# Window attention followed by product-key experts: the layer norms' last step moved from VectorE to ScalarE

## The chip, the cores and the metric

The kernel runs on one core of one Trainium2 chip. The metric is the device time of one execution in microseconds (us). Before the change the median of three runs is 1780.35 us (1779.88 to 1781.02).

## The reference

The input `x` has 16 sequences of 512 tokens of 128 numbers. Two layers are added onto it, each behind a layer norm over the 128 numbers of a token, without weights:

```python
def _layernorm(x, axis=-1, eps=1e-05):
    m = jnp.mean(x, axis=axis, keepdims=True)
    v = jnp.var(x, axis=axis, keepdims=True)
    return (x - m) / jnp.sqrt(v + eps)
...
x = x + _L0_attn_ref(_layernorm(x, axis=-1), L0_attn_w_qkv, L0_attn_w_proj)
x = x + _L0_ffn_ref(_layernorm(x, axis=-1), ...)
```

The first layer is attention with 16 heads of 8 numbers, where each token sees the tokens at most 128 places away. The second normalises its input again over all 8192 tokens (so the statistics of every token are needed before any of it can start), scores two sets of 32 keys for each of 8 heads, takes the eight best sums, and weighs the rows of 1024 experts with them.

## The kernel before, in words

The kernel has two stages. The first, some 830 us, is the attention with both layer norms; the second, the experts, starts when the last sequence's second norm is done. Both norms, and so all of the change, lie in the first stage.

A sequence is called a batch here, with index `b`. It has 4 token blocks (`NQ`) of 128 tokens, one token to a partition, and its heads fall into 4 groups (`NG`) of 4. A unit `n` is one group of one batch. The main loop (L498 to L541) walks through steps `s`: `n, u = divmod(s, 4)`, `b, g = divmod(n, 4)`, so 16 steps to a batch. A step traces:

- `greatest` (L363) for the unit two ahead: four score matmuls into `s_ps` (two PSUM buffers), each followed on VectorE (DVE) by one custom instruction, `masked` (L378), which adds the band mask and takes the row's maximum, `mx`;
- `exponentials` (L407): two pairs of matmuls into `e_ps` (two buffers), each pair followed on ScalarE (ACT) by one Exp into `pT` (L421); GpSimd (POOL) then cuts the sides of the band (L429);
- `weigh` (L435), two steps behind: matmuls of `pT` into `o_ps`;
- at `u == 1` `greatest_rows` (L396: transposes into `mT_ps`, a copy on ACT, a DMA), at `u == 2` `divide` (L453: transposes into `t_ps`, then `rec` and `attn` on DVE), and once a batch `project` (L468);
- one step of the generator `preparing`, which makes the batch two ahead ready: `prepare(b + 2)` (L315) normalises it, transposes it, multiplies it by the q, k and v weights and splits q and k into three bf16 pieces on POOL (`pieces`);
- one step of the generator `beside`, a chain of odd jobs: `ln_stats` of the batches of a later chunk of four (first norm, tiles with "a"), `second_norm` of the last chunk (tiles with "b", from L482), and early on `weights_of_experts`.

`ln_stats` (L271) makes a mean and a variance per token with two DVE instructions a block (L277, L278), then for the whole chunk the square root on ACT (L282) and its reciprocal on DVE (L283). `normalised_T` (L288), called by `prepare` (tiles `xn`) and by `second_norm` (tiles `xi`), does the last step of the norm for the four blocks of a batch with four DVE `tensor_scalar` (L292), yields, transposes them on TensorE (PE) into `ps_m` and copies them out on ACT (L300). The tile `xn` comes from a pool of two buffers that both norms share; `ps_m` is one PSUM buffer which all of `xn`, `xi`, `q`, `k`, `v`, `mT`, `t_ps`, `a_ps` and `y_ps` share. `second_norm` goes on with the statistics `bn_st` over tokens (L488) and a DMA.

What sets the order: matmuls and transposes are kept in program order by `mm` and `tr` (L166 to L171). The instructions of DVE, ACT and POOL in this stage are put in order beforehand by the planner of the framework, which gives an engine, by its own estimate of times, the ready instruction that is earliest in the program; on the chip each engine then runs its list strictly in that order. The waits for data and for free buffers are added to it.

Of the kernel before, what the change touches and what calls it, by code (L numbers as in the profile page):

```python
# [15 lines left out]
AF = mybir.ActivationFunctionType  # L16
ALU = mybir.AluOpType
# [26 lines left out]
def kernel(  # L44
# [13 lines left out]
    nc = tc.nc  # L58
# [3 lines left out]
    NQ = T // P  # L62
# [17 lines left out]
    xs = []  # L80
    for b in range(B):
        t = keep.tile([P, NQ, D], F32, name=f"x_{b}")
# [70 lines left out]
    with ExitStack() as at:  # L153
# [16 lines left out]
        def tr(out, in_, eye):  # L170
            tc.keep_in_program_order(nc.tensor.transpose(out, in_, eye))  # L171
# [99 lines left out]
        def ln_stats(bs, name, into):  # L271

            n = len(bs) * NQ
            mv = ln.tile([P, CH * NQ, 2], F32, tag=f"mv{name}", name=f"mv{name}_{bs[0]}", bufs=3)
            for i in range(n):
                st = ln.tile([P, 6], F32, tag="st", name=f"st{name}_{bs[0]}_{i}", bufs=4)
                nc.vector.bn_stats(st, xs[bs[i // NQ]][:, i % NQ])  # L277
                nc.vector.bn_aggr(mv[:, i], st)  # L278
                if i % NQ == NQ - 1:
                    yield  # L280
            rstd = ln.tile([P, CH * NQ], F32, tag=f"rs{name}", name=f"rs{name}_{bs[0]}", bufs=3)
            nc.scalar.activation(rstd[:, 0:n], mv[:, 0:n, 1], AF.Sqrt, bias=eps)  # L282
            nc.vector.reciprocal(rstd[:, 0:n], rstd[:, 0:n])  # L283
            for i, b in enumerate(bs):
                into[b] = mv[:, i * NQ : i * NQ + NQ], rstd[:, i * NQ : i * NQ + NQ]
            yield

        def normalised_T(b, mv, rstd, dst, tag):  # L288

            xn = w2.tile([P, NQ, D], F32, tag="xn", name=f"{tag}_{b}")  # L290
            for t in range(NQ):
                nc.vector.tensor_scalar(  # L292
                    xn[:, t], xs[b][:, t], mv[:, t, 0:1], rstd[:, t : t + 1],
                    ALU.subtract, ALU.mult,
                )
            yield
            ps = ps_m.tile([P, NQ, P], F32, tag="m", name=f"{tag}_ps_{b}")
            for t in range(NQ):
                tr(ps[:, t], xn[:, t], ident)
            nc.scalar.copy(dst, ps.rearrange("p t q -> p (t q)"))  # L300
            yield
# [13 lines left out]
        def prepare(b):  # L315

            xnT = w2.tile([P, T], F32, tag="xnT", name=f"xnT_{b}")
            yield from normalised_T(b, *norms.pop(b), xnT, "xn")
            for what, w in (("q", wqT), ("k", wkT)):
                ps = ps_m.tile([P, T], F32, tag="m", name=f"{what}_ps_{b}")  # L320
                mm(ps, lhsT=w, rhs=xnT, start=True, stop=True)
                full = w2.tile([P, T], F32, tag="full", name=f"{what}f_{b}")
                nc.scalar.mul(full, ps, 1.0 / math.sqrt(DK) if what == "q" else 1.0)
                yield
                pc = w2.tile([P, 3, T], BF16, tag="pc", name=f"{what}p_{b}")
                yield from pieces(full, pc, f"{what}_{b}")
                via = dr.tile([3, P, T], BF16, tag=f"{what}v", name=f"{what}v_{b}")
                nc.sync.dma_start(via.rearrange("s c t -> c s t"), pc)
                pieced[what, b] = via
            va = vaug[b % 3]  # L330
            if b < 3:
                nc.gpsimd.memset(va, 0.0)
                nc.gpsimd.memset(va[:, :, :, DK : DK + 1], 1.0)
            v_ps = ps_m.tile([P, NQ, NH, DK], F32, tag="m", name=f"v_ps_{b}")
            for t in range(NQ):
                mm(
                    v_ps[:, t].rearrange("p h k -> p (h k)"),
                    lhsT=xnT[:, t * P : (t + 1) * P], rhs=wvT, start=True, stop=True,
                )
            nc.scalar.copy(va[:, :, :, 0:DK], v_ps)  # L340
            yield
# [140 lines left out]
        def second_norm(bs):  # L482
            into = {}
            yield from ln_stats(bs, "b", into)
            for b in bs:
                t = w2.tile([P, T], F32, tag="xiT", name=f"xiT_{b}")
                yield from normalised_T(b, *into[b], t, "xi")
                nc.vector.bn_stats(bn_st[:, b], t)  # L488
                nc.sync.dma_start(xT[b], t)
# [5 lines left out]
        for _ in ln_stats([0], "a", norms):  # L495
            pass
        preparing, beside, ending = iter(()), iter(()), iter(())
        for s in range(-2 * NG * NQ, (NU + 1) * NQ):  # L498
            n, u = divmod(s, NQ)
            b, g = divmod(n, NG)  # L500
            if g == u == 0 and b + 2 < B:
                preparing = prepare(b + 2)
            if g == u == 0 and b == -2:
                beside = chain(ln_stats([1], "a", norms), ln_stats([2, 3], "a", norms))
# [351 lines left out]
    for i in range(NB + 1):  # L856
        b, t = divmod(i, NQ)
# [86 lines left out]
```

## Time and profile before

| | |
|---|---|
| median of 3 runs | 1780.35 us |
| the profiled execution | 1777.3 us |
| its span, first to last instruction | 1775.6 us |
| first stage: up to the end of the last norm | about 836 us |
| PE / DVE / ACT / POOL busy in 60 to 836 us | 666.6 / 589.5 / 479.9 / 398.9 us |
| `tensor_scalar` of L292 | 128 in all, 64 `xn` and 64 `xi` |
| mean duration of those in 60 to 836 us | 452 ns (`xn`), 453 ns (`xi`) |
| ACT table loads at L282 and L421 | 8 and 7, 1.283 us each |

The span is what the profile covers; some 1.7 us of the execution lie around it. From one projection's copy (L475) to the next, batches take 46.5 us when nothing of the second norm runs beside them, 57.2 and 56.7 us in the two windows that hold most of a `second_norm` together with statistics of the next chunk, 48.3 us in the two after those, and 50.6 us in the window with a `second_norm` alone.

A line of the profile that names a group reads: line of the kernel, engine, operation, output<-inputs with their shapes, number of instructions, busy time and mean duration, idle time of the engine in front of them and what ended it. In a timeline a line starts with the start and the length in us; in brackets stands the idle time in front. "xN" means N instructions of a kind in a row.

### The profile page before, as it was taken

The numbers are of one execution on the slowest core, as the hardware profiler recorded it, in microseconds if no ns is written. First come the engines' busy times: TensorE is split into PE (matmuls) and PEld (weight loads), VectorE is DVE, ScalarE is ACT, GpSimd is POOL, SyncE is SP. The second block draws the span as 40 slices with busy tenths as digits, with TensorE's granted clock in tenths as the row PEclk, the third lists the DMA queues.
The fourth block names the chain that finished last, engine by engine and source line by source line (L and its number), as shares of the span: only waits on it lengthen the run. The fifth ranks groups of instructions, "written<-read, shape, count | busy, mean of one in ns | idle before, by whom it ended". The sixth has DMA issues, their size and how long they took to land.

```text
span 1775.6 us, 49257 instructions
## 1 busy us (share of the span) xinstructions
PE 1476.7 (83%) x16752; PEld 856.5 (48%) x16752; DVE 1406.9 (79%) x8087; ACT 1146.9 (65%) x2018; POOL 1035.6 (58%) x1634
## 2 busy tenths in 40 slices
PE   4888887888788888886888888888888887888877
PEld 1444443444344444443455555555555555555555
DVE  6767778877787778775888888888888888888884
ACT  1566666656666566556776767776776767777763
POOL 7455554555555555543566666666666666666664
PEclk9999999999999999998889999999999999999999
DMA  6332222222122222210000000000000000000000
GB/s 176 89 104 70 71 68 66 86 74 70 56 86 74 70 71 78 81 55 25 8 8 14 8 8 14 14 8 8 14 14 14 8 8 14 14 8 8 8 8 14
DMA packets 87565, 75.03 MB, mean 42 GB/s; under 512 B 12177, under 2 KB 83089, under 8 KB 87185
## 3 DMA queue, kind: packets, MB, share of 16 engines
q1 hardware_dynamic: 86480, 71.61, 13.3%
q8 instruction: 133, 2.18, 0.5%
q14 instruction: 120, 0.97, 0.2%
q10 hardware_dynamic: 832, 0.26, 0.1%
HBM read 49.28 MB, written 20.97 MB: 40 GB/s over the span
## 4 chain that ended last, share of the span: by engine, by line
DVE 34%; PE 31%; POOL 16%; ACT 9%; issue 7%; SPq 2%; DMA 1%; DVEq 0%; POOLq 0%; ACTq 0%
DVE masked L378 9%; POOL g L578 6%; PE o_ps L168 6%; DVE idx L578 5%; PE s_ps L168 4%; DVE row L578 4%; PE off_ps L578 4%; PE w_ps L578 4%; PE up_ps L578 3%; POOL word L578 3%; DVE place L578 3%; DVE top L578 3%; ACT pT L421 2%; DVE mine L578 2%; DVE best L578 2%
## 5 line engine op out<-in xcount | busy, mean ns | idle before, releaser
L378 DVE CUSTOM_DVE_ANT_0 masked<-s_ps,band 128x384 bf16<-128x384 f32 (+1 forms) x1024 | 500.3, 489 | 150.0 <-PE s_ps L168 65.7
L421 ACT ACTIVATE pT<-e_ps 128x512 f32<-128x512 f32 (+1 forms) x512 | 357.9, 702 | 239.8 <-PE e_ps L168 224.9
L429 POOL TENSOR_SCALAR_AFFINE_SELECT pT<-pT 128x512 f32<-128x512 f32 x384 | 237.2, 635 | 337.4 <-ACT pT L421 337.4
L168 PE MATMUL s_ps<-kst,qst 128*128 128x384 bf16 (+1 forms) x1024 | 313.6, 307 | 87.2 <-DVE mx L378 66.0
L578 POOL TENSOR_TENSOR cols<-mine,wT 64x512 f32<-64x512 bf16 x256 | 273.0, 1066 | 20.9 <-DVE mine L578 4.0
L578 PEld LDWEIGHTS w_ps<-cols,row 128*64 128x64 f32 x8192 | 248.6, 138 | 25.4 <-POOL cols L578 14.4
L578 PE MATMUL w_ps<-cols,row 128*64 128x32 f32 x8192 | 252.7, 223 | 6.0 <-POOL cols L578 5.0
L578 POOL TENSOR_TENSOR g<-g,gel 128x512 f32<-128x512 f32 x128 | 163.6, 1278 | 151.4 <-ACT g L578 115.3
L168 PE MATMUL e_ps<-qst,kst 128*128 128x384 bf16 (+1 forms) x1024 | 225.3, 303 | 4.1 <-ACT pT L421 4.0
L168 PE MATMUL o_ps<-pT,vaug 128*32 128x384 f32 (+1 forms) x2048 | 191.6, 446 | 5.4 <-POOL pT L429 5.4
L578 ACT ACTIVATE row<-off_p,one 128x512 f32<-128x512 bf16 x256 | 184.8, 722 | 8.3
L578 ACT ACTIVATE off_p<-off_ps 128x512 bf16<-128x512 f32 x256 | 149.0, 582 | 41.6 <-PE off_ps L578 41.6
L578 DVE FIND_INDEX8 idx<-top,sim 128x8 uint32<-128x32 f32 x1024 | 167.3, 210 | 0.0
L168 PEld LDWEIGHTS <-qst 128*128 128x128 bf16 x1024 | 100.8, 99 | 133.0 <-issue 88.1
L168 PEld LDWEIGHTS <-kst 128*128 128x128 bf16 x1024 | 97.2, 98 | 122.9 <-issue 94.7
L578 DVE TENSOR_TENSOR row<-x_ps,nums_p 128x1024 f32<-128x1024 f32 x128 | 151.0, 1228 | 0.0
L578 POOL TENSOR_TENSOR cand<-top 128x512 f32<-128x512 f32 x64 | 68.2, 1066 | 140.1 <-DVE top L578 140.1
L578 PE MATMUL dn_ps<-xt,key_inT 128*64 128x256 f32 x1024 | 133.9, 398 | 17.3 <-ACT off_p L578 16.5
L578 PE MATMUL up_ps<-g,key_out_sb 64*128 64x256 f32 x1024 | 131.4, 398 | 0.0
L578 PE MATMUL off_ps<-p_bf,ident_bf 128*128 128x512 bf16 x256 | 113.9, 445 | 19.4 <-ACT p_bf L578 19.4
L578 DVE TENSOR_TENSOR word<-word,shift 128x128 uint32<-128x128 uint32 x64 | 23.5, 367 | 123.3 <-POOL word L578 123.3
L578 PEld LDWEIGHTS up_ps<-g,key_out_sb 64*128 64x128 f32 x1024 | 97.1, 193 | 44.5 <-issue 34.6
(141 smaller groups left out, 2488.8 us busy)
## 6 DMA issues: line engine op xcount, KB each, us to landing
qst<-qv SPq DMA_DIRECT2D x576, 32.0 KB
kst<-kv SPq DMA_DIRECT2D x576, 32.0 KB
qv<-qp SPq DMA_DIRECT2D x16, 384.0 KB
kv<-kp SPq DMA_DIRECT2D x16, 384.0 KB
x<-in_L_attn_x_dram SPq DMA_DIRECT2D x16, 256.0 KB
xT<-xiT SPq DMA_DIRECT2D x16, 256.0 KB
xt<-xT SPq DMA_DIRECT2D x16, 256.0 KB
out_dram<-o_sb SPq DMA_DIRECT2D x16, 256.0 KB
```

Source lines behind the costliest of these rows:

```text
L168: tc.keep_in_program_order(nc.tensor.matmul(*args, **kw))
L378: nc.vector.tensor_tensor_reduce(masked[:, 0:w], s, band.rearrange("p u k -> p (u k)")[:, from_u : from_u + w], 1.0, LOWEST, ALU.add, ALU. ...
L421: nc.scalar.activation(pT[:, 2 * pair : 2 * pair + 2, 0:w], e_ps[:, :, 0:w], AF.Exp)
L429: nc.gpsimd.affine_select(out=side, in_=side, compare_op=ALU.is_ge, fill=0.0, base=0, pattern=[[0, 4], [sign, P]], channel_multiplier=-sign,)
L578: return lambda *args, **kw: tc.keep_in_program_order(op(*args, **kw))
```

## The change

`ln_stats` gets one more small DVE instruction for a chunk, which makes -mean/std of every token in the place of the means. `normalised_T` lets ACT compute `Identity(x * rstd + shift)` with two per-partition operands in the place of DVE's subtract and multiply, and yields after each two blocks, so that it takes three steps of its generator instead of two. Nothing else changes in the text; what follows a normalisation in `preparing` and `beside` moves back by one step for each.

```diff
             nc.vector.reciprocal(rstd[:, 0:n], rstd[:, 0:n])
+            nc.vector.scalar_tensor_tensor(
+                mv[:, 0:n, 0], mv[:, 0:n, 0], -1.0, rstd[:, 0:n], ALU.mult, ALU.mult
+            )
             for i, b in enumerate(bs):
-                into[b] = mv[:, i * NQ : i * NQ + NQ], rstd[:, i * NQ : i * NQ + NQ]
+                into[b] = mv[:, i * NQ : i * NQ + NQ, 0], rstd[:, i * NQ : i * NQ + NQ]
             yield
...
-        def normalised_T(b, mv, rstd, dst, tag):
+        def normalised_T(b, shift, rstd, dst, tag):
             xn = w2.tile([P, NQ, D], F32, tag="xn", name=f"{tag}_{b}")
             for t in range(NQ):
-                nc.vector.tensor_scalar(
-                    xn[:, t], xs[b][:, t], mv[:, t, 0:1], rstd[:, t : t + 1],
-                    ALU.subtract, ALU.mult,
+                nc.scalar.activation(
+                    xn[:, t], xs[b][:, t], AF.Identity, bias=shift[:, t : t + 1],
+                    scale=rstd[:, t : t + 1],
                 )
-            yield
+                if t % 2:
+                    yield
             ps = ps_m.tile([P, NQ, P], F32, tag="m", name=f"{tag}_ps_{b}")
```

## The prediction, made before the result was known

> **What bounds the kernel now.** All 128 edited instructions lie before 836 us, so I read the page for the engines' sums, then the waits between 60 and 836 us, then DVE's timeline. No engine is full: of these 776 us PE is busy 666.6, DVE 589.5, ACT 479.9. The waits say who holds whom:
>
> ```profile
> ACT pT L421 <- PE e_ps L168: 218.1, 266, 1.9
> ...
> PE s_ps L168 <- DVE mx L378: 60.4, 197, 4.8
> DVE masked L378 <- PE s_ps L168: 56.7, 158, 2.1
> ...
> PE q_ps L168 <- DVE attn L464: 6.8, 13, 0.7
> ```
>
> (waiter, releaser; us in total, times, longest.) PE waits for DVE about as long as DVE for PE: two engines coupled by the two `s_ps` buffers. ACT mostly waits for matmuls; PE waits for ACT little. So an instruction taken off DVE is worth at best its time, and about half of it where the pair alternates; one put on ACT has room.
>
> Next, what a `tensor_scalar` really costs on DVE. The timeline, first two neighbours without one, then two with one in between:
>
> ```profile
> 292.65 0.56 DVE L378 CUSTOM_DVE_ANT_0 masked<-s_ps,band 128x384 bf16<-128x384 f32 x1
> 293.13 0.08 DVE L378 DVE_READ_ACCUMULATOR2_ANT mx<- 128x1 f32 x1
> 293.36 0.56 DVE L378 CUSTOM_DVE_ANT_0 masked<-s_ps,band 128x384 bf16<-128x384 f32 x1
> ```
> ```profile
> 305.69 0.34 DVE L292 TENSOR_SCALAR xi<-x,mvb,rsb 128x128 f32<-128x128 f32 x1
> 305.94 0.54 DVE L378 CUSTOM_DVE_ANT_0 masked<-s_ps,band 128x384 bf16<-128x384 f32 x1
> 306.42 0.08 DVE L378 DVE_READ_ACCUMULATOR2_ANT mx<- 128x1 f32 x1
> 306.42 0.34 DVE L292 TENSOR_SCALAR xi<-x,mvb,rsb 128x128 f32<-128x128 f32 x1
> 306.68 0.54 DVE L378 CUSTOM_DVE_ANT_0 masked<-s_ps,band 128x384 bf16<-128x384 f32 x1
> ```
>
> `masked` follows `masked` after 0.71 us, and after 0.74 us with a `tensor_scalar` between: DVE stands still for some 0.15 us behind every read of the accumulator (293.21 to 293.36) anyway, and the 0.34 us instruction, which overlaps its neighbours, fills that hole. With 256 columns it is 0.58 and 0.60. So a slotted one costs 0.02 to 0.03 us, not the 0.45 us of its mean. Only those cost that are stretched or come in a row.
>
> Quiet batches (46.5 us each) hold no L292 at all: the two `xn` buffers are filled ahead. What is to be gained lies around the second norms. There the chain of the window 255 to 335 us has such a row on it:
>
> ```profile
> 269.17 0.42 DVE masked L378
> 269.59 1.68 DVE xi L292 x5
> 271.27 0.09 DVE mva L278
> ...
> 274.58 0.23 DVE mva L278 x2
> 274.83 0.32 ACT rsa L282
> 275.20 0.13 issue
> 275.34 0.38 DVE masked L378
> ```
>
> For 5.8 us no `masked` runs: five `xi` and the statistics of the next chunk, then the square root on ACT.
>
> **The change part by part.**
>
> *Removed from DVE, fully on the chain:* the row of five, 1.68 us, and its twin at 468.18: 3.4 us. What comes next there is the statistics, which move up by as much.
>
> *Removed from DVE, on the pair:* 14 single ones last 0.56 to 0.75 us, mean 0.69, 0.35 over the 0.34 of the others: 4.9. Four in a row at 105.37 keep `masked` away for 1.96 us from the start of the read, where 0.23 is usual: 1.7. At 308.69 and 506.75 three in a row and one that waits for its buffer keep `masked` away until 312.06; its own matmul starts at 310.69 and takes 0.27, so 1.1 each: 2.2. Some 45 slotted ones by 0.03: 1.3. Together 10.1; as PE and DVE wait for each other equally, half of it counts: 5.0. Bounds: nothing, and all 10.1.
>
> *Added on ACT:* 128 Identities of 128x128 with two per-partition operands. No row has this. From below: Sqrt with a per-partition bias, 128x16, 0.308 us; from above: `xb`, Identity 128x512 with one such operand from SBUF, 0.706 us. A line between these two gives 0.40 at 128 columns; with a second operand that no row shows I take 0.45 (an estimate), so 57.6 us, 48.6 of it for the 108 between 60 and 826 us. ACT is idle for some 296 of 776 us there, which hides most. What is not hidden: ACT starts an instruction each 776/751 = 1.03 us, so 0.45/1.03 = 44% of the 108 delay one that becomes ready meanwhile, by half of 0.45: 10.5 us of delays. ACT stands on the chain for about a tenth (`pT` 5.5%, `mT` 2.3%), and what it delays is partly waited for by PE through `e_ps` and `ps_m`: I let a quarter count, 2.6 us, between a tenth (1.0) and all (10.5).
>
> The Trainium skill, "ScalarE: Activation LUTs", "What ACT_TABLE_LOAD costs", gives 280 ns + 0.833 ns an element with one pointer operand and 93 ns more for a second; an estimate from it is 0.48 us each, 61 us in all and 2.8 for my 2.6. Its "Rules for kernel authors" speaks against the change: additions and multiplications belong on VectorE, which is faster at them. By that rule alone the change loses 128 x (0.48 - 0.34) = 18 us, which would take the sum to 1798; it counts no engine's free time.
>
> *Table loads:* none is added. At 837.52 `xb`'s Identity runs after the Sqrt of `bn_a` at 835.34 with no load between, and `qf`'s scaled copy runs among the Exps.
>
> *Added on DVE:* 11 instructions of at most 128x16, nearest row the reciprocal, 0.18 to 0.25 us. Ten are slotted like the above or stand beside waits: 0.3 us. If that cover is gone, 2.5.
>
> *The end of the stage,* where nothing covers anything:
>
> ```profile
> 831.47 0.18 DVE L283 RECIPROCAL rsb<-rsb 128x4 f32<-128x4 f32 x1 [0.36 <-ACT rsb L282]
> 831.69 1.12 DVE L292 TENSOR_SCALAR xi<-x,mvb,rsb 128x128 f32<-128x128 f32 x4
> 832.15 0.89 PEld L171 LDWEIGHTS xi_ps<-ident,xi 128*128 128x128 f32 x4 [3.32 <-issue]
> ```
>
> Four `tensor_scalar` take 1.12; one small instruction more, a hop to ACT and four Identities at about 0.35 apart take about 0.2 + 0.15 + 1.5. That is 0.7 more, but the transposes run block by block behind them and were the slower part before (the four take 1.15), so I take 0.6 (0.2 to 1.0). At the start of the kernel the same holds for the first `xn`, but there `xnT` stands on ACT behind a square root that ends at 11.09, and POOL's pieces bound what follows: 0.
>
> *Moved:* all behind a normalisation in `prepare` goes one step later: transposes of `xn` from `u=1` to 2, q from 2 to 3, v from 0 to 1, POOL's eight pieces and the two DMAs on SP's queue with them. The last yield is then the 14th of 16 steps, and the loads by `lay` come at the fourth step of the next batch, so no load gets late. At `u=1` `xn` shared `ps_m` with `mT`; now v does. At `u=2` q waited for `attn`; now `xn` does. One collision for one: 0, with 0.5 us a batch either way as bound (the two waits' own means, 0.6 and 0.5), 7 us for 14 batches. `second_norm` of four batches takes 17 steps instead of 13, and the `ln_stats` chained behind it five: 22 of the 24 there are.
>
> *Sum:* -3.4 - 5.0 + 2.6 + 0.3 + 0.6 = -4.9 us. The profiled execution (1777.3, span 1775.6) would take 1772.4; on the median of the runs, which is 3.05 above it, 1775.4.
>
> **The rivals.**
>
> *Nothing to be seen.* Only the rows of five are worth anything (3.4) and the costs of 3.5 eat them: 1780.4. For it: slotted ones are nearly free. Against it: the batches at 48.3 us, with 11 L292 in them, are 1.8 over the quiet ones.
>
> *Slower: ACT waits for the `xn` buffer with Exps queued behind it.* A third tile in a row must wait for PE's transposes of the one before last. On DVE this wait shows as `xn <- PE xi_ps`, 0.31 to 0.64 us, five times in the stage. On ACT `pT` and the copies that free `ps_m` queue behind it, and PE, in its fixed order, comes to those transposes only after the matmuls that need `e_ps` free. At 0.64 for each of the 15 `xi` tiles in the stage it is 9.6 on top: 1785.0. It undoes the gain from 0.33 a tile and shows as slower from 0.57. For it: the planner's times were wrong there already. Against it: PE waits for ACT's `pT` only about 1 us in each of these windows now.
>
> *The step's shift.* v at `u=1` waits for `mT`, and `xn` at `u=2` waits as long as q did, while q meets the projection's copy: one collision more a batch, 0.6 by 14: 1783.8, at the edge of what shows. DVE's and ACT's lists are planned anew as well, so this can come with either sign.
>
> **How the numbers follow.** About 0.2%, 3.6 us, is what a measurement of this kernel can tell from no change. Forecast 0.40, nothing to be seen 0.22, ACT's wait 0.26, the shift 0.12, half of it on each side of the limit. So faster 0.40, same 0.28, slower 0.32. The forecast's own range is 1768 (all 13.5 of DVE, ACT's least) to 1776.8. The range over the cases goes to 1789, where ACT's delays count whole and only the rows of five are gained (1780.35 - 3.4 + 10.5 + 0.9 = 1788.4), and starts at 1767.
>
> **What would show it.** Right: in the profile after, the stretch without `masked` near 270 us is about 1.7 us shorter, the 57 us windows fall by 2 to 4 us, the 46.5 us ones stay, PE's wait for `mx` falls by some 5 us, and the Identities last about 0.45 us without table loads beside them. Wrong: quiet batches change by over 0.5 us (the shift); ACT's L292 group carries idle time ended by PE (the buffer); PE's waits for `pT`, `mT` or `qf` grow by more than 3 us; or the row of statistics in front of the square root grows.

## The result, and the profile after

| | before | after |
|---|---|---|
| median of 12 runs each, us | 1783.49 (1779.30 to 1786.06) | 1783.05 (1777.80 to 1790.62) |
| ratio after/before, 95% interval | | 1.0007 [0.9990, 1.0024] |
| profiled execution, its span, us | 1777.3, 1775.6 | 1784.43, 1782.7 |
| end of the first stage, us | 838.3 | 841.8 |
| DVE busy, ACT busy over the span, us | 1406.9, 1146.9 | 1367.0, 1193.8 |

No change that can be told. The forecast was 4.9 us faster; the work did move, some 40 us of it off DVE and 47 us onto ACT. This is the page's line of the engines after:

```profile
PE 1481.5 (83%) x16752; PEld 858.9 (48%) x16752; DVE 1367.0 (77%) x7970; ACT 1193.8 (67%) x2146; POOL 1036.1 (58%) x1634
```

**A finer measure than the whole time.** Behind the last norm the instruction lists of the two kernels are the same on every engine, so what the change does must show before it. I use the *end of the first stage*: the start of the first matmul into `sim_ps`, at 838.3 us before and 841.8 after. The copies `aT` of the projections cut the stage into a head, 15 windows and a tail. All stage ends below are of one profiled execution of each kernel. A window's length comes back to 0.1 us from one execution to the next, except for the two windows of 57 us. A repeat of the kernel before (one execution, 1780.56 us, nothing edited) shows why those differ:

> The kernel before, once more, for how well the profile's first stage repeats: if the stage is set by the lists alone, it ends within 0.5 us of 838.29 and each window from one projection's copy to the next within 0.3 us of its length.

It measured 836.9 for the stage. Its two long windows take 56.20 and 56.08 us at a mean granted clock of 0.97, where the first execution took 57.17 and 56.71 at 0.94; its other 13 windows agree within 0.02 us, the head differs by 0.8 and the tail by 0.4. So neither half of the expectation held, and the reason is the clock and the two ends. In the tables below a window stands with its clock where that is not 1.00, and a difference between 0.94 and 0.97 (here 1.0 and 0.6 us) needs no edit. What lies behind the stage scatters more: with the same lists it took 937.3 us before, 942.0 in the repeat and 940.9 after.

Windows in us, "first" and "second" being the two that a `second_norm` of four batches runs beside (three such pairs), "last" the last batch, "tail" what follows its `aT`:

| kernel | stage | first, second | first, second | first, second | last | tail |
|---|---|---|---|---|---|---|
| before | 838.3 | 57.17 (.94), 48.30 | 56.71 (.94), 48.35 | 50.61, 46.17 | 33.28 | 11.4 |
| after | 841.8 | 55.37 (.94), 48.34 | 55.77 (.94), 48.73 | 49.59, 48.26 | 36.12 | 12.5 |

The quiet windows are unchanged, 46.5 us. The three first windows are shorter by 1.8, 0.9 and 1.0; one second window is longer by 2.1, the last batch by 2.8, the tail by 1.1, the head by 1.0 (it scatters by up to 2). Summed over all windows, head and tail it is +3.5 us for the stage.

The waits of 60 to 836 us after, for the lines shown of before (waiter, releaser; us in total, times, longest), with one line more:

```profile
ACT pT L425 <- PE e_ps L168: 204.1, 266, 1.9
...
DVE masked L382 <- PE s_ps L168: 80.7, 176, 2.7
PE s_ps L168 <- DVE mx L382: 58.7, 202, 3.6
...
PE xn_ps L171 <- DVE attn L468: 6.3, 13, 0.7
PE e_ps L168 <- ACT pT L425: 5.9, 5, 2.1
```

DVE has less to do and waits for PE 24 us longer (80.7, 56.7 before), while PE waits for `mx` only 1.7 us less (60.4 before; I expected some 5). DVE's freed time became waiting. `xn` now waits for `attn` where `q` did, for as long, as the prediction said.

The row on DVE near 270 us is gone. DVE's timeline after, from the last `masked` of the old group to the next one:

```profile
270.80 0.42 DVE L382 CUSTOM_DVE_ANT_0 masked<-s_ps,band 128x256 bf16<-128x256 f32 x1
...
275.02 0.25 DVE L283 RECIPROCAL rsa<-rsa 128x16 f32<-128x16 f32 x1 [0.85 <-ACT rsa L282]
275.31 0.17 DVE L284 SCALAR_TENSOR_TENSOR mva<-mva,rsa 128x16 f32<-128x16 f32 x1
275.43 0.42 DVE L382 CUSTOM_DVE_ANT_0 masked<-s_ps,band 128x256 bf16<-128x256 f32 x1
```

No `masked` runs for 4.2 us (271.22 to 275.43); before, it was 5.8 (269.59 to 275.34). The stretch is 1.5 us shorter (4.21 for 5.75); some 1.7 was forecast. But it is shorter at its front: its end has not moved. The chain through the same place, followed back from the window's end (start, length, what), tells who holds the end now:

```profile
269.83 0.76 ACT xi L295 x2
270.59 0.49 ACT pT L425
271.08 0.76 ACT xi L295 x2
271.84 1.53 ACT xn L295 x4
273.39 0.87 ACT L282
274.25 0.43 issue
275.43 0.42 DVE masked L382
```

Eight Identities, 3.05 us, stand in ACT's list in front of the table load for the square root, where `xi` was on the chain of DVE before. The Sqrt starts at 274.68 against 274.83.

The Identities themselves, by group, between 60 and 836 us (busy, mean ns; idle time in front of them):

```profile
L295 ACT ACTIVATE xi<-x,mvb,rsb 128x128 f32<-128x128 f32 x64 | 27.5, 491 | 0.4 <-DVE mvb L284 0.4
L295 ACT ACTIVATE xn<-x,mva,rsa 128x128 f32<-128x128 f32 x48 | 20.9, 489 | 0.0
```

0.49 us each where I took 0.45 (and had 0.48 in the estimate beside it), and 0.39 apart in a row (four in 1.65). None waits for a `ps_m` transpose, that is, for its `xn` buffer: the rival "ACT waits for the buffer" did not occur. There are 8 table loads at L282 and 7 at L425, as before.

The end of the stage after:

```profile
834.29 0.18 DVE L283 RECIPROCAL rsb<-rsb 128x4 f32<-128x4 f32 x1 [0.36 <-ACT rsb L282]
834.50 0.16 DVE L284 SCALAR_TENSOR_TENSOR mvb<-mvb,rsb 128x4 f32<-128x4 f32 x1
834.70 1.65 ACT L295 ACTIVATE xi<-x,mvb,rsb 128x128 f32<-128x128 f32 x4 [0.44 <-DVE mvb L284]
```

From the reciprocal to the first `sim_ps` it is 7.54 us after and 6.82 before: 0.7 more, 0.6 was forecast.

### The profile page after: what moved, and what is told of

Its sections match the earlier page's. It is cut to its first block, busy times and chain, and to the rows that moved or that the text cites. A ratio compares the mean times of both kernels' runs of the same rounds, so it can differ in the third digit from the quotient of the medians.

```text
span 1782.7 us, 49265 instructions
## 1 busy us (share of the span) xinstructions
PE 1481.5 (83%) x16752; PEld 858.9 (48%) x16752; DVE 1367.0 (77%) x7970; ACT 1193.8 (67%) x2146; POOL 1036.1 (58%) x1634
## 3 DMA queue, kind: packets, MB, share of 16 engines
q1 hardware_dynamic: 86480, 71.61, 13.5%
## 4 chain that ended last, share of the span: by engine, by line
DVE 32%; PE 31%; POOL 11%; ACT 10%; issue 6%; SPq 5%; DMA 3%; DVEq 0%; POOLq 0%; ACTq 0%
DVE masked L382 9%; POOL g L582 6%; PE o_ps L168 5%; DVE idx L582 4%; PE s_ps L168 4%; SPq L357 4%; DVE row L582 4%; PE w_ps L582 4%; PE off_ps L582 4%; POOL word L582 3%; PE up_ps L582 3%; DVE place L582 3%; DVE top L582 2%; DVE mine L582 2%; ACT pT L425 2%
## 5 line engine op out<-in xcount | busy, mean ns | idle before, releaser
L425 ACT ACTIVATE pT<-e_ps 128x512 f32<-128x512 f32 (+1 forms) x512 | 357.5, 702 | 215.4 <-PE e_ps L168 208.3
L582 PE MATMUL dn_ps<-xt,key_inT 128*64 128x256 f32 x1024 | 137.4, 406 | 17.4 <-ACT off_p L582 16.6
L582 PEld LDWEIGHTS dn_ps<-xt,key_inT 128*64 128x64 f32 x1024 | 69.7, 145 | 100.6 <-ACT off_p L582 44.9
```

Source lines behind the costliest of these rows:

```text
L425: nc.scalar.activation(pT[:, 2 * pair : 2 * pair + 2, 0:w], e_ps[:, :, 0:w], AF.Exp)
L582: return lambda *args, **kw: tc.keep_in_program_order(op(*args, **kw))
```

## The experiments

Theory A: the loss is the step's shift (the second yield). Theory B: it is the Identities, standing in rows before Exps in ACT's list. Theory C: DVE's relief was never worth more than 3 to 4 us. First the two halves of the change, each alone, then the two ends of the scale.

**1. The shift alone** (`tensor_scalar` stays on DVE):

```diff
-            yield
+                if t % 2:
+                    yield
```

> The first stage ends, in the profile, where the first matmul into sim_ps starts: 838.29 us before, 841.79 us after the change. This kernel leaves the last step of the norm on VectorE and only yields after each two blocks. Theory A (the loss is the step's shift): it ends at 840 to 842, and the window of the 13th batch's projection is about 48 us long instead of 46.2. Theory B (the loss is Identities standing in rows in front of Exps on ScalarE): it ends at 838.3 within 1 us.

Measured: 1791.6 us, ratio 1.0059 [1.0037, 1.0081]; stage 850.7, that is 12.4 later than before, and 9 past what theory A said. **The shift alone is slower.** The price does not lie in the quiet batches (46.5 us still).

**2. The engine alone** (Identities, one yield behind the loop as before):

```diff
-                if t % 2:
-                    yield
+            yield
```

> ScalarE makes the last step, but with the one yield of before, so nothing moves by a step. Theory A: the stage ends at 836 to 838, 1 to 4 us earlier than the changed kernel, with the gains at the windows of 57 us kept. Theory B: 840 to 842, with PE waiting for ScalarE's pT by about 3 us in the last batch.

Measured: 1775.7 us, ratio 0.9980 [0.9960, 1.0000]; stage 834.7, 3.6 earlier than before, 7.1 earlier than after, and earlier than theory A's 836 to 838. So on ACT too the shift costs, about 7 us, and without it the swap gains about what whole executions can just not tell.

| kernel | stage | first, second | first, second | first, second | last | tail |
|---|---|---|---|---|---|---|
| shift alone | 850.7 | 58.51 (.94), 50.00 | 58.07 (.94), 51.36 (.97) | 52.15 (.97), 48.00 | 33.48 | 11.9 |
| engine alone | 834.7 | 55.76 (.94), 46.91 | 55.48 (.94), 46.87 | 49.94, 46.02 | 35.46 | 11.7 |

After against engine alone, at the same clocks: the second windows +1.4, +1.9 and +2.2, the first ones -0.4, +0.3 and -0.4. What the shift costs lies in the second windows.

**3. No last step:**

```diff
-            for t in range(NQ):
-                nc.vector.tensor_scalar(...)
...
-                tr(ps[:, t], xn[:, t], ident)
+                tr(ps[:, t], xs[b][:, t], ident)
```

> The last step of both norms is left out: the transposes read x itself, so that neither engine has the 128 instructions and no buffer xn is waited for (the output is that of a kernel without the norms' last step). This is the ceiling of what VectorE's relief can give. The prediction's sum (3.4 of rows on the chain and half of 10.1) says a stage end near 830; theory C (the relief never was worth more than the 3 to 4 us that the 57 us windows gained) says 833 to 835.

Measured: 1763.3 us, ratio 0.9900 [0.9871, 0.9928]; stage 821.7, 16.6 earlier than before, earlier than both expectations. 3.6 of it is the tail, and that is not the worth of four instructions of 1.12 us: the transposes of `x` itself need no statistics either (before, PE waits 3.06 us for the last `xi`; here 0.78 for `x`), and the tail's clock was 0.94 against 0.55. In the windows PE waits for no `xi` or `xn` before, so they are the fairer measure. The windows give 12.8 against before, and 11.1 against the repeat of before, which had this run's clock (0.97) in the long windows. Theory C falls: 11 to 13 us could be had.

**4. The Identities issued twice,** otherwise after:

```diff
+                nc.scalar.activation(
+                    xn[:, t], xs[b][:, t], AF.Identity, bias=shift[:, t : t + 1],
+                    scale=rstd[:, t : t + 1],
+                )
```

> The changed kernel with each Identity made twice into the same tile: 128 more instructions of 0.49 us on ScalarE, some 51 us of its time at a spacing of 0.40. The prediction let a quarter of the delays count, so 2 to 3 us more than the changed kernel (844 to 845). Theory B: over 6 us more (848 or later), most of it in the windows with a second norm and in the last batch. Theory A: under 2 us more.

Measured: 1810.1 us, ratio 1.0181 [1.0151, 1.0211]; stage 869.0, 27.2 later than after, far past theory B's 6. 128 more at 0.385 us apart are some 49 us of ACT; 55% of it came out in the stage, 0.21 us each (a part of it through the clock: the six long windows of this kernel have 0.91 to 0.97). ACT's timeline near the square root, with the rows of the second set between:

```profile
273.21 0.88 ACT L295 ACTIVATE xn<-x,mva,rsa 128x128 f32<-128x128 f32 x2
273.98 0.88 ACT L299 ACTIVATE xn<-x,mva,rsa 128x128 f32<-128x128 f32 x2
274.75 0.88 ACT L295 ACTIVATE xn<-x,mva,rsa 128x128 f32<-128x128 f32 x2
275.52 0.88 ACT L299 ACTIVATE xn<-x,mva,rsa 128x128 f32<-128x128 f32 x2
276.42 1.28 ACT L282 ACT_TABLE_LOAD   x1
```

The load starts 3.0 us later than after (273.39), the whole length of the eight Identities that are made a second time in front of it: here an Identity counts in full. So ACT's idle time hides an Identity in some places and not in others.

Engine alone against the kernel of experiment 3 is 13.0 us of stage (834.7 - 821.7): 3.9 in the tail (which here again holds the wait for the statistics), 8.4 in the windows, 0.7 in the head. The long windows have 0.94 there and 0.97 here, so of the 8.4 some 1 to 2 us are the clock.

**5. The last batches' `xi` on DVE,** otherwise engine alone:

```diff
+                if b < 12 or tag == "xn":
                     nc.scalar.activation(...)
+                else:
+                    nc.vector.tensor_scalar(
+                        xn[:, t], xs[b][:, t], rstd[:, t : t + 1], shift[:, t : t + 1],
+                        ALU.mult, ALU.add)
```

> ScalarE makes the last step with the one yield of before (as in the run with the engine alone, whose stage ends at 834.7 us), but the second norm of the last four batches stays on VectorE, where the last batch lost 2.2 us and the end 0.3 to a row of Identities before Exps. Theory B for the end of the stage (that row is the cause): the stage ends at 832 to 833, 5 to 6 us before that of the kernel before, and the time is 0.3% under it. Rival (the last batch is slow for another reason): 834 to 835.

Measured: 1773.5 us, ratio 0.9957 [0.9941, 0.9974]; stage 832.3, last batch 33.32, tail 11.2. Theory B holds in the last batch, where no scores are left for DVE. ACT and PE in the last batch, first after, then this kernel:

```profile
814.83 2.80 ACT L295 ACTIVATE xi<-x,mvb,rsb 128x128 f32<-128x128 f32 x7
...
817.52 1.07 ACT L425 ACTIVATE pT<-e_ps 128x512 f32<-128x512 f32 x2
818.16 0.48 PE L168 MATMUL e_ps<-qst,kst 128*128 128x384 bf16 x2 [2.15 <-ACT pT L425]
```
```profile
810.34 0.72 PE L168 MATMUL e_ps<-qst,kst 128*128 128x256 bf16 x4
810.77 1.30 ACT L430 ACTIVATE pT<-e_ps 128x512 f32<-128x512 f32 x2 [0.47 <-PE e_ps L168]
```

Seven Identities in a row keep two Exps waiting, and both `e_ps` buffers, and so PE for 2.15 us (in engine alone, behind a row of four, 1.50). Without the row ACT waits for PE instead.

**6 and 7. Which half of the shift?** After, with the second yield kept only for `xn` (6) or only for `xi` (7):

```diff
-                if t % 2:
+                if t % 2 and (tag == "xn" or t == NQ - 1):
```

(and "xi" in place of "xn").

> Both norms on ScalarE; only the first norm (xn, in prepare) yields after each two blocks, so q, k, v and their pieces move by one step in every batch, while second_norm keeps its 13 steps. The shift costs 7.1 us on ScalarE (841.8 against 834.7). Theory S1 (it is the collisions of xn, q and v with the other users of ps_m): the stage ends at 840 to 842. Theory S2 (it is second_norm's longer chain and where its transposes fall): 834 to 836, since the windows without a second norm kept their 46.5 us.

> The counterpart: only the second norm (xi) yields after each two blocks, prepare is as before. Theory S1: the stage ends at 834 to 836. Theory S2: 840 to 842.

| kernel | stage | first, second | first, second | first, second | last | ratio |
|---|---|---|---|---|---|---|
| `xn` shifted | 836.1 | 55.34 (.97), 46.91 | 55.21 (.97), 47.09 | 49.90, 46.83 | 35.45 | 0.9959 [0.9943, 0.9974] |
| `xi` shifted | 837.4 | 55.51 (.94), 46.76 | 55.33 (.94), 46.84 | 49.69, 45.89 | 38.58 (.91) | 0.9982 [0.9956, 1.0009] |

(1772.7 and 1776.9 us.) By its stage end `xn` shifted is as theory S2 said; `xi` shifted is below S2's 840 to 842, and 3.1 us of its distance from engine alone lies in the last batch, at a clock of 0.91. So neither theory holds as it stood. By whole executions `xn` shifted is some 7 us faster than before, though its stage ends only 2.2 earlier; what lies behind the stage scatters by that much in single executions, and the rest of this difference is not explained here. Neither half brings the second windows to the 48.3 to 48.7 of after; it needs both. The waits of `xi`'s transposes on PE give the difference: only in after, in the shift alone and in the kernel with doubled Identities do they wait for `kf`, three times 0.69 us. Of the kernels that shift anything, those are also the three with the longest second windows. (Before has 48.3 in two of its three without that wait; with the last step left out these take 47.0 and 46.9.) A wait for `xnT` came with the shift too, three times 0.68 us in the first windows, but `xn` shifted has it as well and has short second windows. (In before and in the engine alone they wait as long and as often for `qf`, in the first windows; the sum of the waits doesn't tell the kernels apart, the place does.) With both shifts the fourth tile's transposes fall directly behind the k matmuls, and `ps_m` is one buffer: they must wait until ACT has copied k out. That is an association; the next two test it.

**8 and 9. Another place for those transposes.** After, with all of `second_norm` chained one step earlier (8), or with only its fourth tile one step later (9), which makes the chain longer:

```diff
-            if u == 0 and g == 2 and b % CH == 0 and b >= CH:
+            if u == 3 and g == 1 and b % CH == 0 and b >= CH:
```
```diff
             for b in bs:
+                if b % CH == CH - 1 and len(bs) > 1:
+                    yield
```

> The changed kernel with second_norm of the chunks begun one step earlier, so that its transposes fall on other places than those of k and the first of xn. If the shift costs because of the two waits of 0.7 us of xi behind xnT and kf at these places (theory S2a), the stage ends 2 to 4 us earlier than after the change, at 838 to 840. If the place is not what counts but the length of the chain of steps (theory S2b), it stays within 1 us of 841.8.

> The changed kernel with one more step in front of the fourth batch of each second_norm chunk, so that only its transposes move, from the step in which k is multiplied (a wait of 0.69 us for kf) to the next, where mT is. Theory S2a (the place behind k costs): each of the three pairs of windows with a second norm gets 1 to 2.6 us shorter and the stage ends at 835 to 839. Theory S2b (the longer chain costs): the stage ends at 841.8 or later, as the chain is a step longer still.

| kernel | stage | first, second | first, second | first, second | last | ratio |
|---|---|---|---|---|---|---|
| all earlier | 834.7 | 53.46 (.97), 47.56 | 53.63 (.97), 47.74 | 48.43, 47.47 | 37.29 (.95) | 0.9967 [0.9946, 0.9988] |
| fourth later | 837.4 | 54.52 (.97), 47.06 | 54.46 (.97), 47.44 | 49.57, 46.96 | 38.51 (.91) | 0.9998 [0.9979, 1.0016] |

(1775.2 and 1779.8 us.) PE's timeline around the fourth tile, after and in "fourth later":

```profile
327.40 1.02 PE L168 MATMUL k_ps<-xnT,wkT 128*128 128x512 f32 x2
329.12 0.66 PE L171 MATMUL xi_ps<-ident,xi 128*128 128x128 f32 x4 [0.69 <-ACT kf L327]
```
```profile
326.76 1.02 PE L168 MATMUL k_ps<-xnT,wkT 128*128 128x512 f32 x2
327.62 0.33 PE L168 MATMUL s_ps<-kst,qst 128*128 128x384 bf16 x1
...
330.19 0.66 PE L171 MATMUL xi_ps<-ident,xi 128*128 128x128 f32 x4 [0.22 <-ACT mT L407]
```

And the pair of windows there, after and in "fourth later" (stretch, length, busy us and number for PE, PEld, DVE, ACT, POOL, granted clock, DMA share, GB/s):

```profile
256.34:311.71 55.37, 44.93 (x326) 21.53 (x325) 40.44 (x183) 41.06 (x69) 26.02 (x52) 0.94 0.20 62
311.71:360.05 48.34, 42.52 (x326) 20.59 (x325) 35.56 (x147) 34.66 (x62) 26.03 (x52) 1.00 0.28 87
```
```profile
256.55:311.07 54.52, 44.11 (x326) 21.38 (x325) 40.45 (x183) 40.92 (x70) 26.13 (x52) 0.97 0.21 63
311.07:358.13 47.06, 42.17 (x326) 20.60 (x325) 35.54 (x147) 34.41 (x62) 26.07 (x52) 1.00 0.29 89
```

The same instructions, and 1.28 us less in the second window; in the two other second windows it is 1.29 and 1.30, all at clock 1.00. With the longer chain the time came down, as theory S2a said, so it is the place and not the length. It is 3.9 of the 5.8 us that the shift adds to the windows. (All earlier went past S2a's 838 to 840, but it moves all of `second_norm` and shows less.)

PE's own wait shrank by only 0.47 (0.69 to 0.22). The rest shows on DVE, which runs out of scores while PE is at k, waits and transposes. The next `masked` behind k, after and in "fourth later":

```profile
329.97 0.56 DVE L382 CUSTOM_DVE_ANT_0 masked<-s_ps,band 128x384 bf16<-128x384 f32 x1 [1.69 <-PE s_ps L168]
```
```profile
327.98 0.56 DVE L382 CUSTOM_DVE_ANT_0 masked<-s_ps,band 128x384 bf16<-128x384 f32 x1 [0.34 <-PE s_ps L168]
```

Up to there the two executions agree within 0.01 us from the window's start. Then the wait and the four transposes stand in front of PE's next scores, and DVE waits 1.35 us longer for them (1.69 for 0.34; in the two other windows after it waits 1.57 and 1.69); 1.28 of it is left at the window's end. In the whole stage DVE's wait for `s_ps` went from 80.7 to 76.0 us.

**10 to 11. Put together.** "All earlier" with experiment 5's condition (10), and, to be compared with it, with the `xi` of batches 0 to 11 and the `xn` from batch 3 on alone on ACT (11):

```diff
-                if b < 12 or tag == "xn":
+                if (b < 12 if tag == "xi" else b > 2):
```

> The changed kernel with second_norm of the chunks begun one step earlier (whose stage ended at 834.7 us, with 37.3 us in the last batch) and the second norm of the last four batches on VectorE (which took the last batch from 35.5 to 33.3 us). If the two are independent, the stage ends at 830 to 831, 8 us before that of the kernel before, and the time is 0.4 to 0.5% under it.

> As the first of this call, with the first norm of the first three batches on VectorE too, because the head of the stage (up to the first projection's copy) took 112.9 us before and 113.5 to 114.4 with ScalarE. If ScalarE's Identities there are the cause, the head is back at 113 us and the stage ends 1 us earlier than that of the first; if the head follows the planner's order of other work, it ends within 0.5 us of it.

Measured: 1773.5 us, ratio 0.9951 [0.9935, 0.9968], stage 833.4 (830 to 831 was expected; the last batch came as expected, 33.48, the head was 2 longer); and 1769.9 us, ratio 0.9937 [0.9916, 0.9958], stage 830.8. Both are faster than before and than after. What (11) was meant to bring in the head can't be seen (114.2 us; (10) has 116.1, and "all earlier", whose lists there are the same as (10)'s, 114.2): the head scatters more than that.

## Why the prediction was wrong, step by step

- **The bound.** PE and DVE wait for each other, ACT mostly for matmuls: right, and still so after, though less evenly (58.7 and 80.7 us). "As PE and DVE wait for each other equally, half of it counts" was wrong: without the step the windows lose 11 to 13 us, near the 13.5 (3.4 + 10.1) that I had as the upper bound, against the 8.4 that I took.
- **Added on ACT.** I let a quarter of the delays count, 2.6 us, 2.9 with DVE's small instructions. Measured, 8.4 in the windows, some 7 without the clock: nearer to my upper bound of 10.5. What failed is the way of counting. Delays were spread evenly over ACT's list, but the Identities come in rows of 2 to 8 just where `second_norm` releases them, and there ACT is on the chain: in front of the Sqrt (3.05 us on the chain) and, in the last batch, in front of the Exps (2.15 us of PE). The errors of these two terms, 3 to 4 us of gain and 4 to 5 us of cost that I left out, nearly cancel: engine alone gained 3.6 us of stage, and that the -4.9 was not far off for it is luck. (Nor did the loss of 18 us come that the prediction works out from the durations alone.)
- **The row of five:** its place, length and end were right (1.5 shorter for 1.7), its worth was not, since the square root behind it is now held by ACT. The first windows fell by 0.9 to 1.8 us, where I expected 2 to 4.
- **The end of the stage:** 0.7 for 0.6. **Table loads:** none, as said.
- **Moved: this is the step that failed.** I set "one collision for one: 0", and kept 7 us either way as the bound. The list of who shares `ps_m` with whom was right for `xn`, q and v: v waits for `mT` (3.0 us, 14 times), `xn` for `attn`, and q newly for the projection's copy (2.9 us, 12 times). These cost nothing, the quiet batches stay at 46.5. But I shifted only `prepare` and counted `second_norm` as steps of a chain (17 for 13). Its own transposes share `ps_m` as well, and moved against k's matmuls, where the fourth tile costs 1.3 us in each of three windows. The signs of being wrong that I had named watched `prepare` and the buffer, and none of them appeared. The shift cost 7.1 us on ACT and 12.4 on DVE, which is more than the swap gained.
- **The rivals.** The step's shift (forecast 1783.8, given 0.12) has the right cause and sign, and a wrong place: 0.6 a batch by 14, in the quiet batches. "Nothing to be seen" has the outcome for other reasons: more than the rows of five was to be had. ACT's wait for the buffer did not occur.

A sum can be made: the stage moved by -3.6 (engine) + 7.1 (shift) = +3.5 us, 0.2% of the time, inside the interval of the ratio. Of the shift's 7.1 on ACT, 3.9 has the shown cause (the fourth tile behind k); 1.9 more in the windows were not taken apart, and the 1.3 in the head and tail is within what these two scatter. The 12.4 us on DVE were not taken apart either; there the first windows grew too, by 1.3 to 1.5 each.

## What to carry to other kernels

Before an edit adds a step to a generator, list for every user of a single PSUM buffer at which step it comes before and after, and do that for every chain that the edit lengthens, not only for the one in view: one tile put directly behind a long matmul pair cost 1.3 us at each place, though the wait that names it is 0.69. An engine with a third of its time free doesn't hide work that arrives in rows: look at which instruction stands behind the row in its list, and leave on the old engine those parts whose row would stand before chain work (here the last batches). Try the two halves of an edit apart; here one gained 3.6 us of the stage and the other cost 7.1.

## What the runs showed of the hardware

**Behind a short stall of PE the clock can fall to half, and the length of the stall does not decide.** In the last batch the same row of seven Identities holds PE for 1.92 us in "fourth later", 2.00 in `xi` shifted, 2.15 after and 2.21 in "all earlier". The clock fell behind the first, the second and the fourth, and stayed at 1.00 after. In "fourth later" the half clock lasted from about 811.5 to 818.3, some 6.8 us, and the batch took 38.5 us in place of 36.1.

What does decide can be read from the traces. In each execution all changes of the clock lie on one grid of 3.413 us, which starts at another offset in each, and the half clock lasts one, two or more steps of it (3.413, 6.827 us). Cut along its grid, the stall after is split (from 816.01 to 818.16), while the one in "all earlier" (808.49 to 810.70) lies within one step. After, then "all earlier" (the granted clock is third from the end):

```profile
813.06:816.47 3.41, 2.70 (x24) 0.77 (x23) 0.69 (x1) 3.41 (x9) 1.60 (x3) 1.00 0.21 77
816.47:819.88 3.41, 1.72 (x16) 0.91 (x16) 0.00 (x0) 3.23 (x8) 0.64 (x1) 1.00 0.00 0
```
```profile
808.33:811.74 3.41, 1.20 (x13) 0.31 (x11) 0.00 (x0) 3.23 (x8) 0.48 (x1) 1.00 0.00 0
811.74:815.15 3.41, 3.41 (x19) 1.67 (x18) 0.70 (x1) 2.99 (x5) 1.37 (x3) 0.50 0.09 35
```

PE was busy for 1.72 us of the step without a fall, and for 1.20 of the one before the fall (1.75 in "fourth later", at the edge). Over the first stage (70 to 830 us) of all fourteen executions the clock fell from full to half 42 times, each time behind a step of the grid in which PE was busy for less than 1.9 us; every step at full clock with less than 1.7 us had a fall behind it, and none with 1.9 or more had one. So in this kernel the clock falls behind a step in which PE is busy for less than about half, and whether a stall makes such a step depends on where the grid lies. That is also where the 0.94 and 0.97 of the long windows come from: near 280 us the half clock lasts two steps in the first execution of before and one in its repeat. This is read from the traces; no experiment moved the grid.

The Trainium skill, "TensorE: Matmul & The Clock Gate", "What's actually happening", has the clock fall to half after an idle window of about 3.4 us that runs freely. The length and the free run agree with the grid of 3.413 us; idle the steps need not be: PE was busy for up to 1.89 us of them. The same page, "Why this matters for your kernels", wants no idle gaps of TensorE above some 3 us: here the clock fell behind 1.92 already, and the measurement decides.

**An Identity of 128x128 with two per-partition operands** takes 0.49 us alone and 0.39 from one to the next in a row (seven in 2.80, the last of them whole).
